# A two-layer graph network on one Trainium2 core: side products handed out at another pace, eight bursts of gather places for six, and selections of two small groups in one instruction

## The chip, the cores and the metric

The kernel runs on one core of a Trainium2 chip, in one launch. The metric is device time in microseconds (us): 1556.59 us is the median of 7 runs of the kernel before (1553.28 to 1560.29). One more execution was profiled; every duration below comes from it.

## The reference, cut to what matters

There are 6250 nodes with 256 features, and 100,000 edges sorted by destination. The destinations are uneven: `dst` is 6250 times the square of a uniform number, so low-numbered nodes receive far more edges than high-numbered ones. Each of two layers adds, to every node, the rows of the sources of its edges, and puts the sum through a small two-stage network. The input is added at the end and every row is normalised.

```python
def _gin_agg(h, src, dst, eps, n_nodes):
    agg = jax.ops.segment_sum(h[src], dst, num_segments=n_nodes)
    return (1.0 + eps) * h + agg
h = _gin_agg(x, src, dst, eps1, n)
h = jax.nn.relu(h @ W1a + b1a)      # 256 -> 512
h = jax.nn.relu(h @ W1b + b1b)      # 512 -> 512
h = _gin_agg(h, src, dst, eps2, n)
h = jax.nn.relu(h @ W2a + b2a)      # 512 -> 512
out = h @ W2b + b2b                 # 512 -> 256
return _layernorm(x + out, axis=-1)
```

All of it is in 32-bit floating point.

## The kernel before, in words

**Two ways to aggregate.** The edges are cut into 782 chunks of 128, and the nodes into 49 tiles of 128 rows. The first 240 chunks fall on the five lowest tiles (`HEAVY = 5`). For these the kernel doesn't gather rows. In layer 1 it counts how often each source meets each destination (`counting`, L804 on), writes the table of counts to memory, and multiplies it with the feature table. A *product* is one turn of `products` (L743 on): one heavy tile against a range of four node tiles, four matmuls at L784. There are 5 x 13 = 65 products in each layer. Layer 2 reads the counts back (L799) and multiplies them with the output of layer 1.

The other 542 chunks are gathered: GpSimd (POOL) issues one indirect DMA for each chunk (L255), which brings 128 rows to the 128 partitions. A matmul with a 0/1 selection matrix `sel` (L992) adds rows with one destination together in a window of 32 destinations. Chunks are joined in 93 groups of four windows. At a group's end ScalarE copies the group's sums (`split`, L1011), a matmul with a 0/1 matrix `to` (L1023) puts the four windows in their places, and VectorE adds the result to the accumulators of the tiles that the group reaches (L1015). `select` (L590 on) makes `sel` and `to` on VectorE (L598, L603), two groups ahead. The last 63 groups are small: four chunks each (the very last has two), one for each window.

**Places.** Gathered rows wait in on-chip buffers (`early`, in layer 2 also `late`), in *bursts* of four chunks. There are `PIECES = 6` bursts of places. The gathers of burst i + 6 are issued when the matmuls of burst i have been written down, and wait on the chip for the last of them (`last_sum`, L999 on). GpSimd can so be 24 chunks ahead of TensorE. The first six bursts are issued ahead of each layer.

**Blocks.** When a pair of node tiles has all its contributions, it becomes a block: two transposes of the accumulators (L704), four steps of the first network stage (L720), two steps of the second (L734), then the ending on VectorE and ScalarE, and a store. The generator `block` waits three times until its results have been taken from PSUM. The heavy tiles form three blocks, ready only when all the products of their tiles are added.

**The order of the work** is written out by the program before anything runs; each engine follows its own queue in that order. The main loop goes over the groups. After each burst it makes one *tick* for each of its chunks, and at each tick pumps two queues. `blockwise` takes one step of one of the two oldest blocks. `beside` holds the counting and the products; at each tick it gets a credit, `rates[g]`, and gives out work while the credit is above zero (a layer-2 product costs 3.42). `rates` comes from `spread` (L120 on): it distributes `PACES[layer - 1]` times the cost of the side work over the groups, more of it where few blocks fall due, so that side work and blocks together are level. A pace of 1 would give out the last product with the last chunk. What has to be taken from PSUM is taken seven ticks later (`LAG = 7`). After the last chunk, a final loop steps both queues until they are empty.

VectorE is DVE in the profile, ScalarE is ACT, TensorE is PE with its weight loads as PEld, and SyncE's DMA queue is SPq. One 32-bit matmul is two MATMUL records in the trace, so a layer-2 product is eight records.

Of the kernel before, what the change touches and what calls it, by code (L numbers as in the profile page):

```python
# [9 lines left out]
F32 = mybir.dt.float32  # L10
I32 = mybir.dt.int32
AF = mybir.ActivationFunctionType
ALU = mybir.AluOpType
AX = mybir.AxisListType

P = 128
EPS_LN = 1e-5
GRP = 20
PARTS = 4
SLOTS = 32  # L20
BURST = 4
PIECES = 6
HEAVY = 5
RING = 4
W = 10
RANGE = 4
PACES = (1.1, 1.08)
STEP = 0.6
ADD = 0.5
AHEAD = 4  # L30
# [60 lines left out]
def places(N, E, c):  # L91

    chunks = -(-E // P)

    def node(e, side):  # L100
        return N * min(max((e + side * deviation(e, E)) / E, 0.0), 1.0) ** 2

    groups, lo, hi = [], [], []
    while c < chunks:
        n = min(GRP, -(-(chunks - c) // PARTS) * PARTS)
        while n > PARTS and (
            span(N, E, (c + n) * P, n // PARTS * P, SPREAD) > SLOTS
            or span(N, E, (c + n) * P, n * P, SPREAD) > P
        ):
            n -= PARTS  # L110
        groups.append((c, n // PARTS))
        lo.append(int(node(c * P, -1)) // P)
        c += n
        hi.append(min(int(node(c * P, 1)), N - 1) // P)
    return groups, lo, hi


def spread(groups, N, E, work, dense):

    chunks = [min(PARTS * h, -(-E // P) - c) for c, h in groups]
    per = [
        dense * N / P * (min((c + n) * P / E, 1.0) ** 2 - (c * P / E) ** 2) / n
        for (c, h), n in zip(groups, chunks)
    ]
    low, high = 0.0, max(per) + work / sum(chunks)
    for _ in range(60):  # L130
        level = (low + high) / 2
        if sum(n * max(level - p, 0.0) for n, p in zip(chunks, per)) < work:
            low = level
        else:
            high = level
    return [max(high - p, 0.0) for p in per]
# [3 lines left out]
def tile_gin_residual_layernorm(  # L140
# [38 lines left out]
    nc = tc.nc  # L179
# [5 lines left out]
    NCH = -(-E // P)  # L185
    NC, taken = counted(N, E)
    STEPS, END = steps(N, E, taken)
    groups, lo, hi = places(N, E, NC)
    NG = len(groups)
# [23 lines left out]
    iota = const.tile([P, P], F32, name="iota")  # L213
# [19 lines left out]
    members = {}  # L233
# [8 lines left out]

    early = const.tile([P, PIECES * BURST * D], F32, name="early")
    gathered = {}
    last_sum = {}

    def gather(i, table, width, *places):

        if i >= len(pieces):
            return  # L250
        n = PIECES // len(places)
        rows_ = places[i % PIECES // n][:, i % n * BURST * width : (i % n + 1) * BURST * width]
        rows_ = rows_.rearrange("p (c d) -> p c d", d=width)
# [6 lines left out]
        ]  # L260
        if i - PIECES in last_sum:
            together(reads[0], [last_sum[i - PIECES]])
        return rows_, reads

    def together(first, others):

        for o in others:
            tc.add_manual_dep(first.ins, o.ins.name, SYNC, reason="together")

    mask = const.tile([P, KM, NG], F32, name="mask")  # L270
    home = const.tile([P, NG], F32, name="home")
# [4 lines left out]
    with tc.tile_pool(name="prep", bufs=2) as prep, tc.tile_pool(  # L276
        name="prepp", bufs=2, space=bass.MemoryType.PSUM
# [54 lines left out]

        at_first = sorted({c // P * P for i in range(PIECES) for c, _ in pieces[i][1]})
        for c0 in at_first:
# [18 lines left out]
        for i, c in enumerate(range(NC, NCP, 512)):  # L353
            n = min(512, NCP - c)
# [6 lines left out]
        for g0, g1 in runs:  # L361
            c, h = groups[g0]
            n = g1 - g0
# [3 lines left out]
            for j in range(PARTS):  # L367
# [19 lines left out]
                op=ALU.subtract,  # L387
# [49 lines left out]
        for a, b, n in taken:  # L437
# [6 lines left out]
                op=ALU.subtract,  # L444
# [70 lines left out]
    def ordered(ctx):  # L515
# [19 lines left out]
        def layer(number, ctx, table, width, scale, wa, ba, wb, wide, prepare, finish, conclude):  # L535
            kk = width // P
            edge = ctx.enter_context(tc.tile_pool(name=f"edge{number}", bufs=3))
# [14 lines left out]
            sels = {}  # L552
# [35 lines left out]
                    acc[t] = a[:, i, :]  # L588

            def select(g):  # L590
                c0, h = groups[g]
                n = min(PARTS * h, NCH - c0)
                small = h == 1
                sel = edge.tile(
                    [P, PARTS if small else GRP, SLOTS], F32, name="sel",
                    tag="sel1" if small else "sel", bufs=4 if small else 2,
                )
                nc.vector.tensor_tensor(  # L598
                    sel[:, :n, :], iota[:, :SLOTS].unsqueeze(1).to_broadcast([P, n, SLOTS]),
                    slot[:, c0 : c0 + n].unsqueeze(2).to_broadcast([P, n, SLOTS]), op=ALU.is_equal,  # L600
                )
                to = edge.tile([P, P], F32, tag="to", name="to", bufs=6)
                nc.vector.tensor_scalar(to, iota, home[:, g : g + 1], None, op0=ALU.is_equal)  # L603
                sels[g] = sel, to

# [346 lines left out]
            for b in blocks:  # L954
                if b[0] < HEAVY:
                    seed(b)
            due(all=True)
            select(order[0])
            select(order[1])
            blockwise = Queue(4.0, BLOCKS)  # L960
            work = 0.00167 * HEAVY * NT * width
# [3 lines left out]
            else:  # L965
                aside = products([(r, t) for r in range(len(ranges)) for t in heavy],
                                     load_counts)
            rates = spread(
                groups, N, E, PACES[number - 1] * work, 0.00167 * KH * (width + wide)
            )  # L970
# [7 lines left out]
            for k, g in enumerate(order):  # L978
# [5 lines left out]
                c0, h = groups[g]  # L984
                beside.rate = rates[g]
                pm = place(width)
                sel, to = sels.pop(g)
# [44 lines left out]
                if k + 2 < len(order):  # L1032
                    n = len(members[order[k + 1]])
                    later(n // 2 if n > PARTS else 0, lambda k=k: select(order[k + 2]))
# [322 lines left out]
```

## Time and profile before

| | |
|---|---|
| median of 7 runs | 1556.59 us (1553.28 to 1560.29) |
| the profiled execution, its own time | 1554.53 us |
| its span, first to last instruction | 1552.8 us |
| TensorE busy | 1362.6 us (88%), mean granted clock 0.95 |
| GpSimd busy | 1045.4 us (67%) |
| VectorE busy | 708.8 us (46%) |
| ScalarE busy | 390.3 us (25%) |
| moved by DMA | 340.57 MB, mean 219 GB/s |
| gathers | 542 in layer 1 and 542 in layer 2 |
| first gather of layer 1 and of layer 2 | 9.64 us and 765.03 us |
| last gather of layer 1 and of layer 2 | 701.63 us and 1450.87 us |
| last L992 matmul of layer 1 and of layer 2 ended | 712.7 us and 1472.8 us |
| last product (L784) of layer 2 started | 1384.9 us |

Read the table as two layers of the same shape. A layer has a stage in which rows are gathered, and a stretch behind its last gathered chunk in which only blocks are left.

### The profile page before, as it was taken

How to read it: one execution, taken by the hardware profiler on the slowest of the kernel's cores; microseconds unless marked ns; L12 is line 12 of the kernel's file. 1: busy time of each engine (PE TensorE's matmuls, PEld its weight loads, DVE VectorE, ACT ScalarE, POOL GpSimd, SP SyncE). 2: the span in 40 equal slices, each digit the busy share in tenths (PEclk: the TensorE clock that was granted, in tenths of full speed). 3: DMA queues.
4: the chain of work that ended last, by engine and by line, in shares of the span. 5: the costliest groups of instructions: out<-in, count | busy, mean ns of one | idle time of the engine just before them, and what ended most of it. 6: DMA issues, size and time to landing. Idle time of an engine off the chain costs nothing.

```text
span 1552.8 us, 18728 instructions
## 1 busy us (share of the span) xinstructions
PE 1362.6 (88%) x6108; PEld 738.8 (48%) x6108; DVE 708.8 (46%) x2057; ACT 390.3 (25%) x831; POOL 1045.4 (67%) x1098
## 2 busy tenths in 40 slices
PE   2557788888999988999688889999999999999997
PEld 1134454454455445555322244444445555556576
DVE  6954455435556552243112223344445556465633
ACT  0433344222333232232210011111122222222222
POOL 6777777777777777770277777777777777677300
PEclk9779998998999999999789999999999999999999
DMA  6467676675566558741498888889788888778401
GB/s 187 149 215 238 196 252 195 217 230 164 182 191 217 163 171 274 228 142 56 165 313 308 271 259 292 296 290 315 242 298 278 285 285 276 238 234 258 134 27 42
DMA packets 165766, 340.57 MB, mean 219 GB/s; under 512 B 24628, under 2 KB 78110, under 8 KB 165660
## 3 DMA queue, kind: packets, MB, share of 16 engines
q0 software_dynamic: 69376, 213.19, 43.8%
q1 hardware_dynamic: 85776, 109.73, 21.2%
q10 hardware_dynamic: 10508, 16.35, 3.0%
q8 instruction: 52, 0.85, 0.2%
q14 instruction: 54, 0.44, 0.1%
HBM read 303.92 MB, written 35.26 MB: 218 GB/s over the span
## 4 chain that ended last, share of the span: by engine, by line
PE 68%; DMA 11%; POOL 8%; issue 6%; DVE 5%; ACT 1%; DVEq 0%; ACTq 0%; POOLq 0%
PE bank L784 15%; PE bank L720 15%; PE bank L734 14%; PE bank L992 11%; PE bank L1023 9%; POOL early L255 7%; DMA early<-in_x_dram,srcs 6%; PE bank L704 2%; DMA late<-h,srcs 2%; DMA early<-h,srcs 2%; PE bank L869 1%; DMA xr<-in_x_dram 1%; POOL late L255 1%; DVE at L897 1%; DVE at L849 1%
## 5 line engine op out<-in xcount | busy, mean ns | idle before, releaser
L255 POOL DMA_INDIRECT early<-in_x_dram,srcs x542 | 528.2, 975 | 171.2 <-issue 143.2
L784 PE MATMUL bank<-xr,cf 128*128 128x256 f32 (+3 forms) x980 | 361.0, 513 | 22.6 <-issue 14.5
L255 POOL DMA_INDIRECT early<-h,srcs x276 | 262.1, 950 | 150.2 <-issue 71.0
L1015 DVE SCALAR_TENSOR_TENSOR acc<-bank,mask,acc 128x256 f32<-128x256 f32 (+1 forms) x430 | 241.9, 609 | 235.8 <-PE bank L1023 125.8
L255 POOL DMA_INDIRECT late<-h,srcs x266 | 252.6, 949 | 84.4 <-issue 66.1
L784 PEld LDWEIGHTS bank<-xr,cf 128*128 128x128 f32 (+1 forms) x980 | 193.6, 202 | 173.3 <-issue 145.7
L992 PE MATMUL bank<-early,sel 128*32 128x256 f32 (+1 forms) x1636 | 169.0, 489 | 76.1 <-DMA early<-in_x_dram,srcs 54.5
L720 PE MATMUL bank<-zt,w2a_s 128*128 128x256 f32 (+2 forms) x832 | 180.6, 370 | 4.7 <-DVE r L1071 4.7
L1023 PE MATMUL bank<-split,to 128*128 128x256 f32 (+1 forms) x372 | 175.2, 554 | 5.0 <-ACT zt L707 3.2
L734 PE MATMUL bank<-w1b_s,ht 128*128 128x512 f32 (+1 forms) x392 | 177.2, 597 | 0.4 <-ACT ht L724 0.4
L720 PEld LDWEIGHTS bank<-zt,w2a_s 128*128 128x128 f32 x832 | 151.3, 191 | 44.1 <-issue 18.7
L790 DVE TENSOR_TENSOR acc<-bank,acc 128x512 f32<-128x512 f32 (+1 forms) x70 | 46.9, 669 | 218.3 <-PE bank L784 199.7
L1011 ACT COPY split<-bank 128x256 f32<-128x256 f32 (+1 forms) x186 | 88.5, 480 | 218.0 <-PE bank L992 183.5
L833 DVE TENSOR_SCALAR ca<-numbers,low 128x128 f16<-128x128 f16 x240 | 64.0, 267 | 142.9 <-PE bank L869 142.4
L992 PEld LDWEIGHTS bank<-early,sel 128*32 128x32 f32 x1636 | 35.3, 111 | 176.4 <-issue 121.0
L1023 PEld LDWEIGHTS bank<-split,to 128*128 128x128 f32 x372 | 58.1, 195 | 120.8 <-issue 62.7
L734 PEld LDWEIGHTS bank<-w1b_s,ht 128*128 128x128 f32 (+1 forms) x392 | 73.7, 191 | 80.5 <-issue 72.5
L869 PE MATMUL bank<-cb,ca 128*128 128x490 f16 x240 | 83.8, 404 | 23.4 <-DVE cb L836 12.7
L720 PE MATMUL bank<-zt,w1a_s 128*128 128x256 f32 (+2 forms) x416 | 101.1, 383 | 1.4 <-DVE acc L1015 0.8
L849 DVE TENSOR_TENSOR at<-cs,at 128x490 f16 x145 | 75.3, 520 | 50.7 <-ACT cf L857 32.2
L734 PE MATMUL bank<-w2b_s,ht 128*128 128x256 f32 (+1 forms) x392 | 91.7, 382 | 0.7 <-ACT ht L724 0.7
L720 PEld LDWEIGHTS bank<-zt,w1a_s 128*128 128x128 f32 x416 | 78.8, 199 | 20.6 <-issue 4.4
(115 smaller groups left out, 1002.6 us busy)
## 6 DMA issues: line engine op xcount, KB each, us to landing
xr<-in_x_dram SPq DMA_DIRECT2D x60, 512.0 KB, 4.8
counts<-cf SPq DMA_DIRECT2D x60, 256.0 KB, 3.7
cf<-counts SPq DMA_DIRECT2D x60, 256.0 KB, 7.4
h<-h1r ACTq DMA_DIRECT2D x48, 256.0 KB, 2.8
xr<-h SPq DMA_DIRECT2D x12, 1024.0 KB
acc<-h SPq DMA_DIRECT2D x23, 512.0 KB, 7.6
early<-in_x_dram,srcs POOLq DMA_INDIRECT x542
acc<-in_x_dram SPq DMA_DIRECT2D x23, 256.0 KB, 5.1
```

The lines of the kernel that those rows point to most:

```text
L255: nc.gpsimd.indirect_dma_start(out=rows_[:, j, :], out_offset=None, in_=table, in_offset=bass.IndirectOffsetOnAxis(ap=srcs[:, c : c + 1], ...
L720: nc.tensor.matmul(ph[0][:, :nb], wa[:, k, f * P : (f + 1) * P], zt[:, k, :nb], start=(k == 0), stop=(k == kk - 1),)
L734: nc.tensor.matmul(po[0][:m], ht[:, f, i * P : i * P + m], wb[:, f, :], start=(f == 0), stop=(f == KH - 1),)
L784: nc.tensor.matmul(pm[0], cf[:m, j, :], xr[:m, j, :], start=(opens and j == 0), stop=(closes and j == len(ks) - 1),)
L790: nc.vector.tensor_tensor(acc[t], ap, acc[t], op=ALU.add)
L833: nc.vector.tensor_scalar(a, numbers[:, :P], low[:, c : c + 1], None, op0=ALU.is_equal)
L849: nc.vector.tensor_tensor(to, cs.rearrange("p (k w) -> p k w", w=W), to, op=ALU.add)
L869: mm = nc.tensor.matmul(pc[0], a, b, start=(i == 0), stop=(i == n - 1))
L992: mm = nc.tensor.matmul(pm[0][b * SLOTS : (b + 1) * SLOTS], sel[:, c - c0, :], rows_[:, j, :], start=(c == parts[b][0]), stop=(c == parts[ ...
L1011: nc.scalar.copy(split[:used], ap[:used])
L1015: nc.vector.scalar_tensor_tensor(acc[t], ap, mask[:, t - lo[g], g : g + 1], acc[t], op0=ALU.mult, op1=ALU.add,)
L1023: nc.tensor.matmul(pu[0], to[:used], split[:used], start=True, stop=True)
```

## The change

The diff has three parts. `PIECES` goes from 6 to 8, so GpSimd may be 32 chunks ahead, and eight bursts are issued ahead of each layer. `PACES` goes from (1.1, 1.08) to (1.15, 1.4). And `select` handles two successive groups of one chunk per window in one call: one instruction makes both selection matrices, one makes both `to` matrices; the call for the second group then returns at once. For this `to` is made by a `tensor_tensor` with two broadcast operands instead of a `tensor_scalar`, for large groups as well. The buffers are now 3 pairs for small `sel` (4 singles before) and 4 pairs for `to` (6 singles).

```diff
-PIECES = 6
+PIECES = 8
...
-PACES = (1.1, 1.08)
+PACES = (1.15, 1.4)
...
             def select(g):
+
+                if g in sels:
+                    return
                 c0, h = groups[g]
-                n = min(PARTS * h, NCH - c0)
-                small = h == 1
+                gs = [g]
+                if h == 1 and g + 1 < NG and len(members[g]) == PARTS:
+                    gs.append(g + 1)
+                n = sum(len(members[k]) for k in gs)
                 sel = edge.tile(
-                    [P, PARTS if small else GRP, SLOTS], F32, name="sel",
-                    tag="sel1" if small else "sel", bufs=4 if small else 2,
+                    [P, 2 * PARTS if h == 1 else GRP, SLOTS], F32, name="sel",
+                    tag="sel1" if h == 1 else "sel", bufs=3 if h == 1 else 2,
                 )
...
-                to = edge.tile([P, P], F32, tag="to", name="to", bufs=6)
-                nc.vector.tensor_scalar(to, iota, home[:, g : g + 1], None, op0=ALU.is_equal)
-                sels[g] = sel, to
+                to = edge.tile([P, 2, P], F32, tag="to", name="to", bufs=4)
+                nc.vector.tensor_tensor(
+                    to[:, : len(gs), :], iota.unsqueeze(1).to_broadcast([P, len(gs), P]),
+                    home[:, g : g + len(gs)].unsqueeze(2).to_broadcast([P, len(gs), P]),
+                    op=ALU.is_equal,
+                )
+                for i, k in enumerate(gs):
+                    o = groups[k][0] - c0
+                    sels[k] = sel[:, o : o + len(members[k]), :], to[:, i, :]
```

## The prediction

> **What bounds the kernel now.** I read the list of waits first, for who is held up by nothing but itself.
>
> ```profile
> POOL early L255 <- issue: 214.2, 703, 0.3
> PE bank L992 <- DMA early<-in_x_dram,srcs: 54.5, 28, 4.4
> POOL late L255 <- issue: 66.1, 217, 0.3
> POOL early L255 <- DMA h<-h1r: 62.4, 1, 62.4
> POOL late L255 <- PE bank L992: 5.5, 9, 1.8
> ```
>
> The columns are total us, times, longest. GpSimd hardly waits for anybody: 0.3 us of issue before nearly every gather, one hole of 62.4 us between the layers, and little for a place (L992). With a mean of 0.95 us each (950 ns rows of L255) the pitch is 1.25 us per chunk. 542 x 1.25 = 677.5 us is a floor for the gathering of each layer. Second, the timeline of GpSimd at the hole:
>
> ```profile
> 701.63 1.03 POOL L255 DMA_INDIRECT early<-in_x_dram,srcs  x1 [0.30 <-issue]
> 765.03 0.94 POOL L255 DMA_INDIRECT early<-h,srcs  x1 [62.37 <-DMA h<-h1r]
> 766.27 0.95 POOL L255 DMA_INDIRECT early<-h,srcs  x1 [0.30 <-issue]
> ```
>
> So the time is 9.6 of preparation, the gathers of layer 1 (692 to 701.6), a stretch of blocks alone until layer 1's output has landed (63), the gathers of layer 2 (686), and what comes after (102). Third, the engines over stretches of layer 2 (columns: length, PE, PEld, DVE, ACT, POOL busy, clock, DMA share, GB/s):
>
> ```profile
> 763.00:800.00 37.00, 24.42 (x80) 9.61 (x81) 4.34 (x7) 3.92 (x4) 26.49 (x28) 0.82 0.94 341
> 800.00:850.00 50.00, 42.70 (x143) 13.52 (x144) 10.45 (x18) 2.90 (x4) 37.91 (x40) 0.84 0.85 280
> 850.00:900.00 50.00, 39.64 (x136) 13.47 (x136) 11.01 (x19) 2.93 (x5) 37.83 (x40) 0.88 0.88 298
> 900.00:1450.00 550.00, 547.93 (x2369) 287.73 (x2367) 259.99 (x586) 113.17 (x220) 410.81 (x433) 1.00 0.84 272
> 1473.00:1553.00 80.00, 67.19 (x344) 56.03 (x343) 27.37 (x74) 16.48 (x45) 0.00 (x0) 0.96 0.11 34
> ```
>
> TensorE has gaps up to 900, where it waits for gathers at GpSimd's pitch; then it is full while GpSimd also runs at its pitch (433 chunks in 550 us is 1.27): the two are balanced. Behind the last chunk TensorE alone works. Fourth, the timeline of that end, on TensorE:
>
> ```profile
> 1471.76 1.05 PE L992 MATMUL bank<-late,sel 128*32 128x512 f32 x4
> 1472.74 1.13 PE L1023 MATMUL bank<-split,to 128*128 128x512 f32 x2
> ...
> 1482.72 5.34 PE L720 MATMUL bank<-zt,w2a_s 128*128 128x256 f32 x24
> 1488.58 1.99 PE L720 MATMUL bank<-zt,w2a_s 128*128 128x256 f32 x8 [0.52 <-DVE r L1071]
> 1490.41 1.04 PE L704 MATMUL bank<-ident,acc 128*128 128x128 f32 x8
> 1491.29 3.62 PE L734 MATMUL bank<-w2b_s,ht 128*128 128x256 f32 x16
> ...
> 1541.49 1.98 PE L734 MATMUL bank<-w2b_s,ht 128*106 128x256 f32 x8 [0.44 <-ACT ht L724]
> ```
>
> One block is about 12 us of dense TensorE work, and six stand behind the last chunk. Counted in this timeline after 1472.7: 25 first-stage steps, 12 second-stage steps, 10 transposes, 4 placements. The blocks of the five heavy tiles cause part of this: they fall due only when the last product is added.
>
> **Pace of layer 2, the large part.** Nothing is added; 65 products are moved. By `spread` the rate per tick goes from 0.632 to 0.756 at the start and from 0.345 to 0.469 where it is least; adding credits chunk by chunk (five products are given out ahead of the loop), the last product comes with chunk 707 at pace 1.08 and 575 at 1.4. The first agrees with the trace: gather 707 issues near 1358 us, the last L784 starts at 1384.9. A block is 8 steps and three waits of 8 ticks, some 32 ticks, and two are in hand, so one block leaves per 16 ticks. Blocks fall due every 22 chunks near 575 and every 17 near 710. Three heavy blocks at 707 can't be worked off any more; at 575 they can. Following those rules tick by tick leaves 25, 12 and 10 steps behind the last chunk at 1.08, just what the timeline has, and 16, 8 and 6 at 1.4. A step of either stage is 8 records, 1.73 us (3.46 for 16 in the chain of waits), a transpose 0.44: 9 x 1.73 + 4 x 1.73 + 4 x 0.44 = 24.3 us leave the end.
>
> They come back among the chunks, and the question is what they push. I sum TensorE's work per 64 chunks by those counts, with 0.25 per chunk (L992, 1.0 for four), 0.97 per placement (L1023) and 3.43 per product (8 records in the chain), against GpSimd's 80 us:
>
> chunks 240, 304, 368, 432, 496, 560, 624, 688, last 30
> before 42.9, 67.3, 80.6, 80.7, 77.4, 88.0, 86.3, 89.8, 35.6 (sum 648.6)
> after 49.8, 77.6, 87.4, 90.9, 84.3, 91.5, 74.8, 76.6, 37.8 (sum 670.7)
>
> TensorE ends a stretch at the later of its own sum and GpSimd's time plus 6 us (issue to landing, 6 in the chain near 795). Before: 851, 931, 1012, 1092, 1171, 1259, 1345, 1435, 1470.7 (the trace has 1472.8). After: 851, 931, 1018, 1109, 1194, 1285, 1360, 1437, 1474.3. So of 22.1 us moved in, 18.5 fill gaps (17.2 of them in the first 128 chunks, where the trace has gaps of 30 us in 137) and 3.6 show. Layer 2: 3.6 - 24.3 = **-20.7 us**.
>
> **Pace of layer 1.** The same count: the last product moves from chunk 719 to 691, and behind the last chunk 2 second-stage steps (8 records of 128x512, 3.43 us each) and a transpose (0.25) fewer are left: -7.1 us of 43.5 (712.7 to 756.2, all TensorE). Among the chunks its work rises from 541 to 548 us against GpSimd's 677; only chunks 656 to 687 are over the pitch (49.6 to 40), and the next 32 take that back (32.3). Layer 1: **-7 us**, all that it moves being hidden under GpSimd.
>
> **Eight bursts.** Two bursts more ahead of each layer are no new gathers: GpSimd went on to its 25th at 40.28 us without a pause. In layer 2 GpSimd's last gather starts 9.6 us later than 541 pitches after its first (1450.87 to 765.03 + 676.25), in six waits between 1293 and 1380, where TensorE is 20 to 30 us behind and 24 places are worth 30. After, TensorE is up to 40 us behind (1285 to 1245 at chunk 624) and 32 places are worth 40, so GpSimd waits 5 to 10 us again, ends near 1449, and its last rows land some 19 us ahead of need. With six bursts it would end near 1456. Value: 0, bounds -3 and +1.
>
> **Selections.** Per layer 63 small groups cost 0.279 (`sel`, 128 wide) + 0.294 (`to`), 36.1 us; after, 31 pairs at 2 x 0.416 (the row of `sel` at 256 wide) and one single, 26.4: 10 us per layer less on VectorE, which is busy 260 of 550 us; TensorE waited 1.2 us in all for `to` in layer 2. Value 0, bounds -1 and 0. A rule speaks against it: the Trainium skill, "VectorE: DVE Perf Modes", section "The perf-mode tier table", gives an fp32 `tensor_scalar` twice the rate of a `tensor_tensor`. By that rule `to` loses 64 of 128 cycles at 0.96 GHz, 67 ns (an estimate) for each of 30 large groups, 4 us of VectorE in both layers. By the rows they are equal (280 ns median for `to`, 279 mean for a `sel` of that size); I take the rows. The pair's later release of `to` and `sel` buffers adds a VectorE wait for TensorE; the matmul it waits for was written down 11 or more ticks earlier, and VectorE's other work waits for results 7 ticks old, so it is already met. Were it not, the adds at L1015 and the PSUM banks behind them would wait.
>
> **Queues and DMA.** Each moved product takes its loads with it: 256 KB of counts and a fifth of 1024 KB of h on SP's queue. 65 x 461 KB = 30 MB pass in some 415 us instead of 585, so 21 GB/s more beside 280 to 311 up to 1180. That is below 341, moved at a DMA share of 0.94. SP also holds the seeds (L577) and stores (L1096), in order. Value 0, because no L784 waited for h or counts in layer 2; bound +40, see below.
>
> **Clock.** At 800 to 900 the clock is 0.84 to 0.88, and 97 records of L784 take 49.6 us, 41.6 at full rate. The Trainium skill, "TensorE: Matmul & The Clock Gate", section "Why this matters for your kernels", puts this down to idle gaps over 3 us. By the rule, filled gaps would return these 8 us; by the row, TensorE waits there for gathers and what it saves becomes gap. I take 0 and give the low end 8.
>
> **Sum.** -20.7 - 7.1 = -27.8 us. The profiled execution (span 1552.8, own time 1554.53) becomes 1526.7. The median stands 2.06 above it: **1529 us**.
>
> **The rivals.**
> *The filling fails* (25%). TensorE is 547.9 of 550 us busy from 900 on; if the gaps before 900 don't take the 17 us (products at the front wait for their loads), what leaves the end of layer 2 returns in the middle. Layer 2 then gives between 0 and -10: 1539 to 1550. For it: DMA is at 0.85 to 0.94 there, and 14.5 of the 30 us of gaps are one wait ahead of a product (L784, in the list of waits). Against: the waits there are for gathers, which a product before them doesn't delay.
> *Late operands* (10%), the slower case. In layer 2 a product's counts or h arrive late through SP's queue, and TensorE, which follows its order, stands with gathers and blocks behind it. A load of counts takes 7.4 us (median) and 15.9 at most. The gain is used up at 28/65 = 0.43 us for each product; at 1 us each the time is 1529 + 65 = 1594, at 0.6 us 1568. Against: four count buffers and two of h.
> *More than counted* (10%): the 8 us of clock and 3 of GpSimd on top, 1516 to 1522.
> *The pace does nothing* (5%): blocks stay behind the last chunk because hands, not products, limit them; 1554 to 1559.
> My forecast (50%) is 1522 to 1537.
>
> **How the numbers follow.** About 0.2%, 3.1 us, can be told from no change. Faster: 50 + 25 + 10 = 85%, less 1 for the edge; same 5; slower 11. The range takes in the forecast, the gain at its largest and the failed filling: 1516 to 1550; the late operands and no effect stay out.
>
> **What would show it.** The last product of layer 2 starts near 1190 instead of 1385; 16 first-stage steps follow the last L992 matmul, and that stretch to the last L734 is 47 us, not 71; the last L992 matmul ends 711 to 712 us after layer 2's first gather, 707.8 before; that first gather comes near 758, not 765. Wrong would be: L784 waiting for `xr<-h` or `cf<-counts`, GpSimd's pitch above 1.25 in layer 2's first half, or a last L992 over 20 us later.

## The result, and the profile after

The changed kernel takes 1546.01 us (median of 13 runs, 1537.73 to 1553.19) against 1556.48 us (34 runs) for the kernel before: a ratio of 0.9935, interval 0.992 to 0.9949, or 10.5 us faster. The forecast was 27.8 us. Its profiled execution took 1544.67 us, with a span of 1542.8, 10.0 less than before.

In the new listing every line behind `select` stands 11 higher: L992 is now L1003, L720 L731, L734 L745, L784 L795, L1023 L1034. The timeline of GpSimd at the hole between the layers:

```profile
704.28 0.95 POOL L255 DMA_INDIRECT early<-in_x_dram,srcs  x1 [0.30 <-issue]
767.55 0.95 POOL L255 DMA_INDIRECT early<-h,srcs  x1 [62.33 <-DMA h<-h1r]
```

Layer 2's first gather starts at 767.55 us, 2.5 us later than before; the forecast had it 7 us earlier. A single execution can't tell 2.5 us: in eight of the experiments below that keep layer 1's pace at 1.1, on chips of about the same speed, this gather starts between 764.2 and 769.1 us. But no 7 us were gained. So layer 1 gave nothing that can be told, and layer 2 all: from its first gather to the end of the span it took 775.3 us, 787.8 before. The engines over the same stretches as before, the last one cut at the new end (length, PE, PEld, DVE, ACT, POOL busy, clock, DMA share, GB/s):

```profile
763.00:800.00 37.00, 23.54 (x80) 9.29 (x80) 4.35 (x7) 4.37 (x5) 24.68 (x26) 0.82 0.89 325
800.00:850.00 50.00, 42.77 (x148) 14.49 (x148) 9.68 (x16) 2.32 (x3) 37.95 (x40) 0.93 0.90 306
850.00:900.00 50.00, 44.49 (x165) 15.64 (x162) 14.49 (x25) 3.51 (x6) 38.02 (x40) 1.00 0.86 283
900.00:1450.00 550.00, 547.44 (x2425) 295.77 (x2425) 257.62 (x536) 118.04 (x232) 414.26 (x433) 1.00 0.84 273
1473.00:1543.00 70.00, 57.24 (x285) 45.51 (x283) 25.79 (x67) 12.88 (x35) 0.00 (x0) 0.94 0.10 31
```

Between 800 and 900 TensorE runs 313 matmul records where it ran 279, at a clock of 0.93 and 1.00 for 0.84 and 0.88: the front did fill. From 900 to 1450 it is as full as before with 56 records more. Then the end of layer 2, on TensorE:

```profile
1448.80 1.07 PE L1003 MATMUL bank<-early,sel 128*32 128x512 f32 x8
1449.80 1.12 PE L1034 MATMUL bank<-split,to 128*128 128x512 f32 x2
1454.18 1.07 PE L1003 MATMUL bank<-early,sel 128*32 128x512 f32 x8 [3.26 <-ACT zt L718]
1455.17 1.74 PE L1034 MATMUL bank<-split,to 128*128 128x512 f32 x2
1456.70 3.01 PE L731 MATMUL bank<-zt,w2a_s 128*128 128x256 f32 x8
...
1485.05 1.05 PE L1003 MATMUL bank<-late,sel 128*32 128x512 f32 x4
...
1531.54 1.98 PE L745 MATMUL bank<-w2b_s,ht 128*106 128x256 f32 x8 [0.44 <-ACT ht L735]
```

Behind the last L1003 matmul stand 47.4 us of TensorE work (70.7 before), with 16 first-stage steps, 8 second-stage steps and 6 transposes, as forecast. But that matmul ends 718.6 us after the layer's first gather (forecast 711 to 712, before 707.8), and ahead of it is a hole of 3.26 us, behind which the same instructions run slower (1.74 us for the two records of L1034 that took 1.12, 3.01 for eight of L731 that take 1.89): the granted clock is 0.50 from 1455.6 to 1459.0.

### The profile page after: what moved, and what is told of

The parts are those of the page before. It is cut to its first block, busy times and chain, and to the rows that moved or that the text cites. A ratio compares the mean times of both kernels' runs of the same rounds, so it can differ in the third digit from the quotient of the medians.

```text
span 1542.8 us, 18581 instructions
## 1 busy us (share of the span) xinstructions
PE 1352.7 (88%) x6108; PEld 733.7 (48%) x6108; DVE 703.8 (46%) x1933; ACT 391.4 (25%) x831; POOL 1053.2 (68%) x1098
## 4 chain that ended last, share of the span: by engine, by line
PE 67%; DMA 12%; POOL 7%; DVE 6%; issue 5%; ACT 2%; DVEq 0%; ACTq 0%; SPq 0%; POOLq 0%
PE bank L745 15%; PE bank L731 15%; PE bank L795 15%; PE bank L1003 10%; PE bank L1034 8%; POOL early L255 6%; DMA early<-in_x_dram,srcs 4%; DMA xr<-in_x_dram 2%; DMA late<-h,srcs 2%; PE bank L715 2%; PE bank L880 1%; POOL late L255 1%; DMA early<-h,srcs 1%; DMA acc<-h 1%; DVE at L908 1%
## 5 line engine op out<-in xcount | busy, mean ns | idle before, releaser
L795 PE MATMUL bank<-xr,cf 128*128 128x256 f32 (+3 forms) x980 | 349.5, 500 | 29.6 <-issue 14.6
L255 POOL DMA_INDIRECT late<-h,srcs x270 | 257.9, 955 | 85.9 <-issue 70.7
L795 PEld LDWEIGHTS bank<-xr,cf 128*128 128x128 f32 (+1 forms) x980 | 188.4, 196 | 171.7 <-issue 140.2
L1003 PE MATMUL bank<-early,sel 128*32 128x256 f32 (+1 forms) x1628 | 164.6, 482 | 59.0 <-DMA early<-in_x_dram,srcs 40.7
L731 PE MATMUL bank<-zt,w2a_s 128*128 128x256 f32 (+2 forms) x832 | 181.4, 372 | 5.4 <-DVE r L1082 3.1
L745 PE MATMUL bank<-w1b_s,ht 128*128 128x512 f32 (+1 forms) x392 | 177.7, 599 | 1.8 <-ACT ht L735 1.8
L1034 PE MATMUL bank<-split,to 128*128 128x256 f32 (+1 forms) x372 | 173.7, 550 | 5.2 <-ACT zt L718 2.7
L731 PEld LDWEIGHTS bank<-zt,w2a_s 128*128 128x128 f32 x832 | 152.7, 193 | 43.3 <-issue 14.2
L1034 PEld LDWEIGHTS bank<-split,to 128*128 128x128 f32 x372 | 56.8, 192 | 121.1 <-issue 59.7
L745 PEld LDWEIGHTS bank<-w1b_s,ht 128*128 128x128 f32 (+1 forms) x392 | 73.9, 192 | 83.4 <-issue 73.2
L731 PE MATMUL bank<-zt,w1a_s 128*128 128x256 f32 (+2 forms) x416 | 105.4, 393 | 5.0 <-DVE acc L1026 2.9
L1003 PEld LDWEIGHTS bank<-early,sel 128*32 128x32 f32 x1628 | 35.2, 111 | 157.0 <-issue 112.5
L731 PEld LDWEIGHTS bank<-zt,w1a_s 128*128 128x128 f32 x416 | 80.9, 204 | 28.8 <-issue 7.7
L735 ACT ACTIVATE ht<-bank,b2a_s 128x256 f32<-128x256 f32 (+2 forms) x104 | 43.5, 458 | 194.1 <-PE bank L731 193.5
```

What stands on the lines that cost most here:

```text
L255: nc.gpsimd.indirect_dma_start(out=rows_[:, j, :], out_offset=None, in_=table, in_offset=bass.IndirectOffsetOnAxis(ap=srcs[:, c : c + 1], ...
L731: nc.tensor.matmul(ph[0][:, :nb], wa[:, k, f * P : (f + 1) * P], zt[:, k, :nb], start=(k == 0), stop=(k == kk - 1),)
L745: nc.tensor.matmul(po[0][:m], ht[:, f, i * P : i * P + m], wb[:, f, :], start=(f == 0), stop=(f == KH - 1),)
L795: nc.tensor.matmul(pm[0], cf[:m, j, :], xr[:m, j, :], start=(opens and j == 0), stop=(closes and j == len(ks) - 1),)
L1003: mm = nc.tensor.matmul(pm[0][b * SLOTS : (b + 1) * SLOTS], sel[:, c - c0, :], rows_[:, j, :], start=(c == parts[b][0]), stop=(c == parts[ ...
L1034: nc.tensor.matmul(pu[0], to[:used], split[:used], start=True, stop=True)
```

## The experiments

Twelve kernels were run. Three terms of every trace are used: the time from a layer's first gather to its last selection matmul (L992, L1003), the *lag* of that matmul's end behind the start of its own gather, and TensorE's work behind it.

**One part alone.** Four kernels take one part each over into the kernel before.

```diff
-PACES = (1.1, 1.08)
+PACES = (1.1, 1.4)      (e1_pace2)
+PACES = (1.15, 1.08)    (e2_pace1)
-PIECES = 6
+PIECES = 8              (e3_pieces)
```

The fourth, e4_select, takes over the new `select`.

> The kernel before with the pace of layer 2 at 1.4 and nothing else (six bursts, old selections, layer 1 at 1.1). Theory A (layer 2's pace is worth less than summed, because the end of the gathering stage has stalls that the sum of TensorE's work doesn't hold, and layer 1's pace is worth nothing): 10 to 13 us below the kernel before, 1544 to 1547. Theory B (the paces are worth what was summed, 21 us here, and selections or places take it back): 1534 to 1537. With six bursts theory A expects GpSimd's last gather of layer 2 later than in the changed kernel by some 7 us, without a loss at the end.

> The kernel before with the pace of layer 1 at 1.15 and nothing else. Theory A: no gain, 1555 to 1559; the last L992 matmul of layer 1 comes some 6 to 9 us later after the first gather (703 before) and eats the 6 to 7 us that are saved behind it. Theory B: 7 us faster, 1549 to 1550, the last L992 matmul of layer 1 unmoved.

> The kernel before with eight bursts of places for six and nothing else. Theory A: 0 to -2 us, 1554 to 1557, GpSimd's waits for places in layer 2 (9.6 us) gone. Theory B: slower by 3 to 10 us.

> The kernel before with the selections of two small groups in one instruction and nothing else. Theory A: 0, 1555 to 1558, VectorE's busy time about 20 us lower less what it gains in waiting. Theory B: slower by 3 to 10 us, with TensorE waiting for sel or to, or VectorE waiting for L992 before sel.

Measured against 1556.09 us for the kernel before: layer 2's pace 1545.12 us (0.9932, 0.9907 to 0.9957); layer 1's pace 1559.79 (1.0023, 1.0009 to 1.0038); places 1552.93 (0.9981, 0.9969 to 0.9993); selections 1557.17 (1.0008, 0.9995 to 1.0021). Theory A holds, though two of its ranges were missed by about 1 us (layer 1's pace above 1559, places below 1554). Layer 2's pace alone is the whole result, layer 1's pace costs 4 us alone, eight bursts alone give 3 (the low bound of the prediction), and the pairs give nothing that can be told. GpSimd's *excess* is the time from its first to its last gather beyond 541 pitches of 1.25 us. With places alone, its excess in layer 2 falls from 9.6 to 2.1 us, so that was the wait that they remove. With layer 2's pace alone and six bursts it grows to 20.7 us (10.9 in the changed kernel), and no loss in time can be told.

**The hole at the end of layer 2.** The chain of the changed kernel and ScalarE's timeline show what TensorE waited for. The chain:

```profile
1436.98 3.47 PE bank L731 x16
1440.48 0.22 ACT ht L735
1440.69 12.15 DMA acc<-h
1452.89 0.05 issue
1452.93 0.72 ACT acc L584
1453.65 0.48 ACT zt L718
1454.13 0.04 issue
1454.18 1.07 PE bank L1003 x8
```

ScalarE:

```profile
1441.20 0.59 ACT L1022 COPY split<-bank 128x512 f32<-128x512 f32 x1
1452.93 0.72 ACT L584 ACTIVATE acc<-acc,e 128x512 f32<-128x512 f32 x1 [11.14 <-DMA acc<-h]
1453.56 0.57 ACT L718 COPY zt<-bank 128x512 f32<-128x512 f32 x1
1454.02 0.59 ACT L1022 COPY split<-bank 128x512 f32<-128x512 f32 x1
1454.50 0.60 ACT L718 COPY zt<-bank 128x512 f32<-128x512 f32 x1
1454.98 0.61 ACT L1022 COPY split<-bank 128x512 f32<-128x512 f32 x1
```

The last accumulator's seed (a tile of 106 rows) is issued at 1440.69 and takes 12.15 us to land. Its scaling on ScalarE was written down five ticks behind the load. ScalarE follows its queue in order, so for 11.14 us it stands there, and four copies out of PSUM, two `zt` and two `split`, come behind. TensorE works off what it has and then lacks a bank. The experiment writes the scaling down later, and nothing else:

```diff
-                later(5, lambda: nc.scalar.activation(
+                later(14, lambda: nc.scalar.activation(
```

> The changed kernel with the scaling of a seeded accumulator on ScalarE (L584) written down 14 ticks after its load instead of 5, so that ScalarE doesn't stand in its queue until the last seed (12 us) has landed. Theory C (the stall at the end of layer 2 is ScalarE held by a late seed): TensorE's wait of 3.26 us for zt near 1454 us and the slow clock behind it go, the last 26 chunks of layer 2 take 37 to 39 us instead of 42.2, the time falls by 3 to 5 us, to 1541 to 1543. Theory D (the last 26 chunks are long only because they hold more and wider block steps): within 1 us of the changed kernel, 1545 to 1547.

It took 1536.26 us, 0.9881 (0.9866 to 0.9895) of the kernel before, measured beside it (1554.58). The changed kernel is at 0.9935: another 0.54%, about 8 us (5 to 12 by the two intervals), more than expected. TensorE and ScalarE of e5_seed at the same place:

```profile
1449.66 3.62 PE L745 MATMUL bank<-w2b_s,ht 128*128 128x256 f32 x16
1453.21 1.07 PE L1003 MATMUL bank<-early,sel 128*32 128x512 f32 x8
1454.21 1.12 PE L1034 MATMUL bank<-split,to 128*128 128x512 f32 x2
1455.26 1.06 PE L1003 MATMUL bank<-early,sel 128*32 128x512 f32 x8
1456.26 1.12 PE L1034 MATMUL bank<-split,to 128*128 128x512 f32 x2
1457.22 1.89 PE L731 MATMUL bank<-zt,w2a_s 128*128 128x256 f32 x8
```

```profile
1450.34 0.59 ACT L1022 COPY split<-bank 128x512 f32<-128x512 f32 x1
1460.74 0.30 ACT L1093 ACTIVATE sd<-mv,lneps 128x2 f32<-128x2 f32 x1 [9.81 <-DVE mv L1086]
1460.95 0.71 ACT L584 ACTIVATE acc<-acc,e 128x512 f32<-128x512 f32 x1
```

No hole, no slow records, and L584 no longer waits. The last 26 chunks of layer 2 take 37.2 us instead of 42.2, and the lines account for all of it: 3.26 of hole, 0.62 and 1.12 of slow records. This repeats. With pace 1.4 and early scaling, all four traces have the hole (3.26, 3.40, 3.25 and 4.75 us in the changed kernel, e1_pace2, and e6 and e7 below) and 42.1 to 44.5 us for these chunks; with late scaling, e5_seed and two kernels below (e9, e10) have none and 37.2 each. Theory C is right.

Why the median gains about 8 us and not 5 is not shown. The profiled execution of e5_seed was the slowest of its four (1542.55 us), with a layer 1 that ended 5 us later, so its span is only 2.0 us shorter. From first gather to the end of the span its layer 2 takes 768.2 us instead of 775.3. But 1.7 us of this lie behind the last chunk (45.7 for 47.4), and they are not late scaling's: e1_pace2 and e6, which have the hole, take 45.7, and e10, which hasn't, takes 47.4. There TensorE waits 1.61 us for `zt` in all of them, and in some of them its clock falls behind that wait:

```profile
1495.87 8.86 PE L731 MATMUL bank<-zt,w2a_s 128*128 128x256 f32 x32 [1.61 <-ACT zt L718]
```

This is the changed kernel; in e5_seed the same 32 records take 7.17 us behind the same wait.

The same edit in the kernel before:

> The kernel before with only the scaling of seeds (L584) written down 14 ticks after the load instead of 5. If the stall by the last seed is made by layer 2's new pace (in the kernel before, ScalarE waits as long but its copies at that place are not next on TensorE's path): within 2 us of the kernel before, 1553 to 1557. If early scaling costs the kernel before as much: 6 to 9 us faster, 1546 to 1549.

1556.06 us, 0.9994 (0.9981 to 1.0007): nothing that can be told. In the kernel before, ScalarE waits at the same L584, and TensorE for 1.78 us. In order, ScalarE and TensorE of the kernel before:

```profile
1451.68 0.72 ACT L584 ACTIVATE acc<-acc,e 128x512 f32<-128x512 f32 x1 [9.47 <-DVE st L1074]
```

```profile
1452.93 1.12 PE L1023 MATMUL bank<-split,to 128*128 128x512 f32 x2 [1.78 <-ACT split L1011]
```

The profile names VectorE as what ended ScalarE's wait. But the seed's last packet is moved at 1451.1, 0.6 us ahead of L584, just as in the changed kernel (1452.4 and 1452.93), so I take it as the same wait. In the trace of e8_before_seed TensorE's 1.78 us are gone, and the last 26 chunks take 29.2 us for 31.0. The wait is old; that it decides some 8 us is new with the pace.

**Layer 1's pace.** Two more paces in the changed kernel:

```diff
-PACES = (1.15, 1.4)
+PACES = (1.1, 1.4)      (e6_pace1_back)
+PACES = (1.35, 1.4)     (e7_pace1_135)
```

> The changed kernel with layer 1's pace back at 1.1. If the effects add up (layer 1's pace alone cost 3.7 us): 3 to 4 us faster than the changed kernel, 1541 to 1543. If the loss belongs to the single change alone: 1545 to 1547.

> The changed kernel with layer 1's pace at 1.35. Theory E (1.15 loses because it puts the last products into chunks 656 to 691, where TensorE can't make the lag good before the end; work behind the last chunk is the same 37 us from 1.15 on): the products end near chunk 615, the lag of TensorE at chunk 755 falls back to 13 us or less, and the time is 6 to 11 us below the changed kernel, 1535 to 1540. Theory F (any faster pace in layer 1 loses, through VectorE's counting work and GpSimd's pitch): 1547 to 1555, GpSimd's excess over 1.25 us per gather in layer 1 above 22 us in all (19 in the changed kernel).

1544.19 us at 1.1 (0.9941, 0.9921 to 0.9962) and 1547.6 at 1.35 (0.9943, 0.9921 to 0.9964): neither can be told from the changed kernel's 0.9935. Theory E had the fall of the lag right (at 1.35 it is 6.8 us at chunk 755) and the time wrong, and the work behind the last chunk too (41.5 us for its 37). Theory F's time was met and its sign was not: GpSimd's excess in layer 1 is 19.6 us, no more than in the changed kernel (19.0). The traces say why, in us:

| | lag at chunk 691 | at 755 | at the last chunk | TensorE behind it |
|---|---|---|---|---|
| pace 1.1, before | 15.6 | 12.6 | 11.1 | 43.5 |
| 1.1, e6_pace1_back | 16.4 | 14.5 | 12.6 | 43.5 |
| 1.15, e2_pace1 | 26.9 | 17.1 | 20.6 | 37.3 |
| 1.15, changed kernel | 24.8 | 14.1 | 17.1 | 37.3 |
| 1.15, e5_seed | 29.7 | 17.3 | 20.0 | 37.3 |
| 1.35, e7_pace1_135 | 18.0 | 6.8 | 11.6 | 41.5 |

Lag and work behind add up to 54.6, 56.1, 57.9, 54.4, 57.3 and 53.1; all nine traces at pace 1.1 on chips of about the same speed lie between 54.0 and 56.2. In TensorE's timeline one sees where the two second-stage steps went that no longer stand behind the last chunk. First the kernel before, then e2_pace1:

```profile
712.07 0.63 PE L992 MATMUL bank<-early,sel 128*32 128x256 f32 x4
712.62 0.70 PE L1023 MATMUL bank<-split,to 128*128 128x256 f32 x2
713.16 0.38 PE L704 MATMUL bank<-ident,acc 128*128 128x128 f32 x2
713.38 3.60 PE L734 MATMUL bank<-w1b_s,ht 128*128 128x512 f32 x8
716.81 0.59 PE L1023 MATMUL bank<-split,to 128*128 128x256 f32 x2
717.24 3.60 PE L734 MATMUL bank<-w1b_s,ht 128*128 128x512 f32 x8
```

```profile
710.17 0.64 PE L992 MATMUL bank<-early,sel 128*32 128x256 f32 x8 [1.36 <-DVE acc L1015]
...
713.79 0.64 PE L992 MATMUL bank<-early,sel 128*32 128x256 f32 x8 [2.13 <-ACT ht L724]
714.36 0.70 PE L1023 MATMUL bank<-split,to 128*128 128x256 f32 x2
714.90 0.53 PE L704 MATMUL bank<-ident,acc 128*128 128x128 f32 x2
715.22 8.62 PE L734 MATMUL bank<-w1b_s,ht 128*128 128x512 f32 x16
723.77 0.63 PE L992 MATMUL bank<-early,sel 128*32 128x256 f32 x4
```

Sixteen records of L734, two steps, stand between the last burst and the one ahead of it. The last gather started at 703.84, so its rows were used 20 us later. Work was moved across the line at which I cut my sum, on an engine that was behind on both sides of it. In e2_pace1 half of the added lag, 4.5 us, stands at chunk 755 already (17.1 for 12.6). The other half comes in the last 26 chunks. As every step came forward, these hold as many steps as before (four of each stage), and still they take 36.1 us for 31.0: TensorE waits 1.36 us for VectorE and 2.13 us for ScalarE, and behind that the two steps take 8.62 us, 7.03 elsewhere. The changed kernel has it too (waits of 1.36 and 1.74, then 8.07 us).

**The best version.** Four kernels combine these: late scaling and pace 1.1 in layer 1 (e9_seed_pace1_back); late scaling in layer 2 alone (e10_seed_layer2); that with layer 2 at 1.6 (e11_pace2_16); and layer 2's pace with late scaling in layer 2, without any other part of the change (e12_pace2_seed_alone).

```diff
+                later(14 if number == 2 else 5, lambda: nc.scalar.activation(
+PACES = (1.1, 1.6)      (e11_pace2_16)
```

> The changed kernel with late scaling of seeds in both layers and layer 1's pace back at 1.1. If layer 1's pace costs 4 to 5 us wherever it stands (first gather to the end of the hole: 756 at pace 1.1, 761 at 1.15): 1531 to 1534, against 1536 with pace 1.15. If layer 1's pace is without effect: 1535 to 1538.

> As the one before (pace 1.1 and 1.4), with the late scaling in layer 2 alone. If late scaling acts only through layer 2's last seed: the same time within 1.5 us as with late scaling in both. If it holds layer 1 up (its stage was 2.7 to 5 us longer in the run with late scaling in both): 2 to 4 us faster than with both.

> As the one before, with layer 2's pace at 1.6 for 1.4. By the count the products end at chunk 531 and 2 second-stage steps and 2 transposes fewer stay behind the last chunk, 4.4 us: 2 to 5 us faster than at 1.4 if TensorE makes its lag good by chunk 755; the same or slower if GpSimd's waits for places (40 us and more of lag near chunk 500) delay the last gathers past TensorE's need.

> The kernel before with layer 2's pace at 1.4 and late scaling of seeds in layer 2, and nothing else: six bursts of places, old selections, layer 1 at 1.1. If these two lines hold the whole gain of the best versions (0.9881 to 0.9892 of the kernel before) and the eight bursts and the pairs add nothing beside them: 1537 to 1540, and TensorE's last 26 chunks of layer 2 in 37 us. If eight bursts are needed once the stall is gone (with six, GpSimd's last gather came 11 us later after the first, 696.9 against 685.8 before): 1542 to 1547.

Against 1556.37: 1538.78 us (0.9892, 0.9873 to 0.9911), 1539.36 (0.9888, 0.987 to 0.9906) and 1540.99 (0.9899, 0.9881 to 0.9917). All overlap with e5_seed's 0.9881: no difference can be told between late scaling in layer 2 alone and in both, nor between layer 1's two paces. The hoped-for 1531 to 1534 of the first did not come. At 1.6 the steps behind the last chunk are fewer as counted (6 second-stage steps for 8, 4 transposes for 6), but the stretch hardly is (45.6 us for 47.4), for it has a wait of 3.52 us. TensorE's lag reaches 48.5 us at chunk 499, beyond 32 places, the last gather comes 701.8 us after the first for 688.7 at 1.4, and TensorE waits once for counts (3.9 us). The last kernel ran on a chip on which the kernel before took 1783.99 us; there its ratio is 0.9898 (0.9861 to 0.9936). In its trace a gather follows the one before it after 1.51 us in layer 1 and 1.45 in layer 2 (mean; 1.28 and 1.27 in the changed kernel), so the balance is another one, and the interval is too wide to say whether eight bursts help beside the late scaling.

## Why the prediction was wrong, point by point

Two steps failed. What the moved work of layer 2 pushes among the chunks was summed as 3.6 us and took 10.8; and the 7 us of layer 1, counted as hidden under GpSimd, were not gained.

- **What bounds the kernel**: right. The pitch stayed (687.1 us from the first to the last gather of layer 2, 685.8 before), and layer 2 without its stall takes 767.4, 768.2 and 770.0 us in three traces, 17.8 to 20.4 less than before, for the 20.7 forecast.
- **Steps that leave the end of layer 2**: right. Counts met, 23.3 us for the 24.3 in the sum.
- **What they push among the chunks**: failed, in the last term. The sum gave 3.6 us; measured 10.8 (718.6 less 707.8). Up to chunk 755 it held: that matmul ends 676.4 us after the first gather, 676.8 before, and at chunk 371 it is 175.0 in both, so the gaps took the early products as forecast. In the last 26 chunks the stretch grew from 31.0 to 42.2 us; 2.2 us were in the sum for the last 30. Part is a size: before, four of the first-stage steps there belong to the one-tile heavy block and are half as wide (0.97 for 1.73 us, 3.0 us for the four), which I costed alike. The other part, 5.0 us, is ScalarE held by the last seed, a wait that the prediction gave no price, though the list of waits of before has its kind (ScalarE's L584 for `acc<-h`, 77.1 us in 10 waits): the step "TensorE ends a stretch at the later of its own sum and GpSimd's time" leaves out that its results must be taken away. e5_seed measures it at about 8 us of the median, of which its trace shows these 5.0.
- **Layer 1's -7 us**: failed. The 6.2 us behind the last chunk did go (43.5 to 37.3), but the claim that the work moved ahead of it is "hidden under GpSimd" did not hold: TensorE was already 11 us behind the last gather, 5 more than landing takes, and I let it recover at a rate it does not have. For chunks 691 to 781 of e2_pace1 my costs give 91 us; it took 107.5, with 8.7 idle, against GpSimd's 114. The lag at the last chunk rose by 6 to 9.5 us and took the gain back: by moved steps, and by two waits and slow records, for which the sum had no term.
- **Eight bursts**: within its bounds. -3 alone, nothing that can be told beside pace 1.4, as argued there: GpSimd's waits don't count while TensorE is far behind.
- **Selections**: right in time. VectorE's two lines fell from 118.1 to 98.2 us in e4_select, as summed, but its whole busy time only from 708.8 to 700.1. `to` took 283 ns for 128 columns as a `tensor_tensor` and 418 for 256; the rule that it should lose to `tensor_scalar` isn't seen in the time or the row.
- **Clock**: the rule was right that filled gaps bring the clock back (0.84 and 0.88 to 0.93 and 1.00), the row was right that this is no gain there: TensorE stood at the same point at chunk 371.
- **Queues and DMA**: right. No L795 waited for h or counts at pace 1.4; DMA reached 0.90 of its time at 306 GB/s. Of GpSimd's excess of 10.9 us, only 3.4 were waits for places (two, of the 5 to 10 us forecast); some 7 were gathers longer than 0.95 us, which stays unexplained.
- **The rivals**: "the filling fails" had the size (1539 to 1550 holds 1546), not the place; the front filled, and the end and layer 1 failed, so its size is luck. "Late operands" had the right kind of cause, a queue that stands in order behind a late transfer, at the wrong queue: ScalarE's seed, not SP's products.
- **A sign that I misplaced**: the last product of layer 2 started at 1230.3 us, not 1190; I had left TensorE's own lag out of it.

Why layer 1's pace costs 4 us alone and nothing that can be told beside the other parts stays open; the sums above put the three traces at 1.15 between -0.2 and +3.3 us of the kernel before, where an unchanged pace scatters from -0.6 to +1.6.

## What to carry to other kernels

When work is moved ahead of the last item of a producer, ask how far the consumer is behind that item: a consumer that is behind has no cover there, and a step moved across the line only changes its side. A sum of one engine's work also needs the engines that empty its results: look for instructions in their queues that wait for a DMA, and place them so late that the data has landed. Such a wait can stand in the profile before at no cost and decide the time as soon as the path moves.

## What the runs showed of the hardware that was not expected

The last seed, 106 rows of 2 KB (212 KB), took 11.5 to 13.1 us from issue to landing in four runs (12.15, 12.30, 11.53, 13.11), while seeds of 128 partitions with 512 KB took 7.0 us (median). The Trainium skill, "DMA: Bandwidth & Descriptors", section "Why a DMA increments its semaphore by 16 and not by 1", says that a transfer issued as this one spreads over the largest number of engines up to 16 that divides the slowest dimension of both its sides; for 106 that is two. The packets in the trace of the changed kernel agree: the seed's 106 packets of 2 KB, 99 ns each (mean), lie between 1443.1 and 1452.2 us, at most two at a time but for 0.2 us, and two packets of 4 bytes close them, where the load of 128 partitions issued just before is closed by sixteen. At that page's 27 GiB/s for each engine two would need some 4 us (an estimate), so it doesn't explain the 9 us, and no run here gave the seed another shape.

The clock does not fall behind every wait alike. Behind the holes of 3.25 to 3.40 us ahead of the last bursts, the granted clock was 0.50 for 3.4 us in all three traces. Behind the wait of 1.61 us after the last chunk it was 0.50 for 3.4 us in the changed kernel, e7 and e10, and stayed at 1.00 in e1_pace2, e5_seed, e6 and e9: 1.7 us of time that no edit made. The 3 us of the rule in the prediction is so no safe bound for these waits.
